# A four-layer kernel on one core: output buffers, the place of the first unit's scans, and the place of layer 2's image copies

## The chip, the cores and the metric

The kernel runs on one core of one Trainium2 chip. Times are microseconds on the device, from the core's first to its last instruction, and the metric is the median over runs. The engines are TensorE (PE in the profile; PEld is its loading of weights), VectorE (DVE), ScalarE (ACT), GpSimd (POOL) and SyncE (SP), which here only issues DMAs. Each engine works through its own instructions in the order of the program; semaphores make one wait for another.

## The reference

The input is float32, two images of 64 channels and 96 x 96 pixels. Four layers follow one another:

- Layer 0: attention over all 9216 pixels of an image with 1x1 convolutions around it, then a batch norm and the residual.
- Layer 1: two depthwise convolutions (3x1 and 1x3) and the input summed, a 1x1 convolution, batch norm and relu; then a layer norm over channels and one Mamba block over the sequence of all 9216 pixels, and a residual.
- Layer 2: Mamba blocks over short sequences of 96 pixels, first down the columns and then along the rows, each forward and backward, with an RMS norm ahead and a joining linear map and residual after.
- Layer 3: a 3x3 filter per group of channels, whose weights come from the image's mean through a tanh, and the residual.

The Mamba block is the core of it, for 128 inner channels and 16 states each:

```
x, z = split(in_proj(norm(u)))
x    = silu(causal_conv4(x) + conv_b)
dt, B, C = split(x_proj(x));  dt = softplus(dt_proj(dt) + dt_b)
h[t] = exp(dt[t] * A) * h[t-1] + dt[t] * B[t] * x[t]      # 128 x 16 states
y    = (sum over states of h * C  +  D * x) * silu(z)
out  = out_proj(y)
```

## The kernel before, in words

The whole image stays on the chip in two tiles, `xa` and `xb`, of 128 partitions (2 images x 64 channels) and 9216 elements. Layer 0 (`layer0_direct`) uses both; afterwards `xb` is the image that layers 1 and 2 read and write in place, and the start of `xa` is carved up (`Carver`) for small tables.

Layers 1 and 2 are one stream of *units* (`layers1_2` builds the list, `Mamba.run` emits it). A unit is one Mamba block over 768 pixels. Layer 1 has 24 units: 12 pieces of each image, one after the other, and the state is carried from piece to piece (`u.carry`). Layer 2 has 96: 24 pairs for the columns, then 24 pairs for the rows; a pair is the forward and the backward block on the same eight sequences. The pair shares its norm, which belongs to the first unit (`u.norm.unit is u`), and one output matmul, `tail`, which belongs to the second. In both layers the first unit of a pair is an even one, counted from 0, and the second an odd one.

A unit has 16 *steps* of scans. The 128 x 16 states are dealt out as 16 turns of 128 rows; a step takes two turns of half a unit, 384 pixels. For one step:

- `read` (L846) fetches `spread`: two DMAs of 384 KB from `rows` in device memory, where `step_write` (L825) put `dt` and `dt * x`. It is issued five steps ahead.
- `decay` (L853) makes `h = exp(dt * A)`, two ACT instructions, three steps ahead.
- `inputs` (L863) makes `dt * x * B` on DVE into a PSUM tile `place`; two steps' `inputs` are issued together at the even step.
- `scan` (L878 in layer 2, L874 in layer 1) is DVE's scan; then GpSimd multiplies by `C` (L879).
- `gather` (L888; L885 begins each half) adds the turns into the PSUM tile `y` on PE, two or three steps later.

`B` is one PSUM tile for half a unit. `shared` (L857) makes it on PE: at step 6 for the second half of the unit, and at step 14 for the first half of the next. It waits until the last `inputs` of the old half has read the tile, and the next `inputs` waits for it.

Everything else of a unit is a *piece*, and the table `PIECES` is an order written out by hand: (offset, name) puts the piece `offset` steps after the unit's step 0. Offsets of -51 to -6 make ready for the scans, 10 to 27 come after. So at each step the program has pieces of up to five units, and offset modulo 16 is the step at which a piece stands. Within a step come the fetch, the decay, the inputs, scan, `B`, gathers, then the pieces that read PSUM (`reads`), then the others. The pieces that matter here:

- `norm_square` at -49 (step 15): in layer 2 two ACT copies of the image (L714, one for each half of the partitions) and ACT's square of the copy (L715); in layer 1 the square and one copy of a matmul's result. `norm_mean` at -47 (step 1) is PE's mean of it (L693), and needs the PSUM tile `mm` that most pieces share.
- `silu` at -22 (step 10), with a table load on each side; `step_mm` at -21 (step 11); `step_read` at -19, `step_exp` at -18, ACT's pieces of the softplus; GpSimd's `step_kept`, `step_sum`, `step_dt` and `step_u` from -17 to -9 (L806 to L816), and `step_write` at -6.
- `c_read` at -15 (step 1): ACT takes `C` out of `mm` (L832).
- `y_half` at 10 and `y_read` at 18: ACT copies a half of `y` into the output tile `yg` (L892, L895); `yg` has two buffers. `y_gate` at 19 multiplies by the gate on GpSimd (L898).
- `tail_0` and `tail_1` at 25 and 26 (steps 9 and 10): PE's output matmuls, which read `yg` of both units of the pair, one half each; `tail_read` at 27 (step 11) writes the image (L921, L924).

The first unit's preparing pieces are emitted ahead of the table (`if offset < 0` in `run`), with layer 1's first relu chunks (`first`, L199 and L200). The table then starts at step -51 of the first unit, so pieces of units 1, 2 and 3 stand ahead of the first unit's scans.

`other` hands out, two calls to each unit at steps 3 and 5, the rest of layer 1's relu chunks and the preparation of layer 2's weights (`mamba_weights`, `joined`).

Of the kernel before, what the change touches and what calls it, by code (L numbers as in the profile page):

```python
# [19 lines left out]
FP = mybir.dt.float32  # L20
# [5 lines left out]
P = 128  # L26
# [45 lines left out]
def setup(ctx, tc, x, cols, mats, dtw):  # L72

    nc = tc.nc
    const = ctx.enter_context(tc.tile_pool(name="const", bufs=1))
    big = ctx.enter_context(tc.tile_pool(name="big", bufs=1))
    k = SimpleNamespace(tc=tc, nc=nc, const=const)

    k.mats = const.tile([P, NMAT], FP, name="mats")
    k.cols = const.tile([P, NCOL], FP, name="cols")  # L80
    k.dtw = const.tile([DT_RANK, NMAMBA * P], FP, name="dtw")
    first = MAT_AT["g_b"][1]
    nc.scalar.dma_start(out=k.mats[:, :first], in_=mats[:, :first])
    nc.scalar.dma_start(out=k.cols, in_=cols)
    nc.scalar.dma_start(out=k.mats[:, first:], in_=mats[:, first:])
    nc.scalar.dma_start(out=k.dtw, in_=dtw)
    k.xa = big.tile([P, L], FP, name="xa")
    k.xb = big.tile([P, L], FP, name="xb")


    half, step = L // 2, L // 6
    own, other = rows_of(0), rows_of(1)
    for i in range(0, half, step):
        nc.sync.dma_start(out=k.xa[own, i : i + step], in_=x[own, i : i + step])
        nc.sync.dma_start(out=k.xb[other, half + i : half + i + step], in_=x[own, half + i : half + i + step])
    nc.sync.dma_start(out=k.xa[other, :half], in_=x[other, :half])
    nc.sync.dma_start(out=k.xb[own, half:], in_=x[other, half:])
    nc.sync.dma_start(out=k.xa[:, half:], in_=x[:, half:])

    k.ident = const.tile([P, P], FP, name="ident")  # L100
    make_identity(nc, k.ident)

    k.mean_c = const.tile([P, P], FP, name="mean_c")
    nc.vector.memset(k.mean_c, 0.0)
    for b in range(B):
        nc.vector.memset(k.mean_c[rows_of(b), rows_of(b)], 1.0 / C)

    k.mean = const.tile([P, 1], FP, name="mean")
    nc.vector.memset(k.mean, 1.0 / C)
    k.mean = k.mean.to_broadcast([P, P])  # L110
    k.eps = const.tile([P, 1], FP, name="eps")
    nc.vector.memset(k.eps, EPS)
    k.minus = const.tile([P, 1], FP, name="minus")
    nc.vector.memset(k.minus, -1.0)

    k.col = lambda name, rows=slice(0, P): k.cols[rows, COL_AT[name][0] : COL_AT[name][1]]
    k.mat = lambda name, rows=slice(0, P): k.mats[rows, MAT_AT[name][0] : MAT_AT[name][1]]
    return k
# [409 lines left out]
def mamba_tables(k, pool):  # L528

    nc = k.nc
    G = P // 8
    t = SimpleNamespace()

    t.member = pool.tile([P, 8], FP, name="member")
    nc.vector.reduce_sum(t.member, k.ident.rearrange("p (g i) -> p i g", i=8), axis=AX.X)
    t.group = pool.tile([P, 2, G], FP, name="group")
    for j in range(2):
        nc.vector.reduce_sum(t.group[:, j], k.ident.rearrange("p (g i) -> p g i", i=8), axis=AX.X)  # L540

    t.turned = pool.tile([P, G, G], FP, name="turned")
    two = t.group.rearrange("p j g -> p (j g)")
    for n in range(G):
        nc.vector.tensor_copy(t.turned[:, n], two[:, G - n : 2 * G - n])

    pair = pool.tile([P, 2, P], FP, name="pair")
    nc.vector.tensor_copy(pair, k.ident.unsqueeze(1).to_broadcast([P, 2, P]))
    pair = pair.rearrange("p j c -> p (j c)")
    t.gather = [pair[:, P - 8 * n : 2 * P - 8 * n] for n in range(G)]  # L550

    t.centre = pool.tile([P, 2, C], FP, name="centre")
    for j in range(2):
        nc.vector.tensor_add(t.centre[:, j], k.ident[:, :C], k.ident[:, C:])
        nc.vector.tensor_scalar_add(t.centre[:, j], t.centre[:, j], -1.0 / C)
    t.centre = t.centre.rearrange("p j c -> p (j c)")
    return t


def scratch(t, pool):  # L560

    t.placed = pool.tile([P, D_STATE, 8], FP, name="placed")
    t.rates = pool.tile([P, P // 8, P // 8], FP, name="turned_rates")


def mamba_weights(k, w, pool, product, tables, i):

    nc = k.nc  # L570
    G = P // 8


    a = pool.tile([P, D_STATE], FP, name=f"A{i}")
    nc.scalar.activation(a, k.col(f"A_log{i}"), AF.Exp)
    nc.vector.tensor_scalar_mul(a, a, -1.0)
    nc.vector.tensor_mul(
        tables.placed,
        tables.member.unsqueeze(1).to_broadcast([P, D_STATE, 8]),
        a.unsqueeze(2).to_broadcast([P, D_STATE, 8]),  # L580
    )
    p = product(tables.placed.rearrange("p s i -> p (s i)"), tables.group[:, 0], P, G)
    yield
    nc.vector.tensor_mul(tables.rates, tables.turned, p.unsqueeze(1).to_broadcast([P, G, G]))  # L584
    w.rates = pool.tile([P, G], FP, name=f"rates{i}")
    nc.vector.reduce_sum(w.rates, tables.rates, axis=AX.X)
    in_w = k.mat(f"in_w{i}")
    if i:
        nc.vector.tensor_scalar_mul(in_w, in_w, k.col(f"norm_w{i}"))
    yield  # L590
    conv_w = k.col(f"convd_w{i}")
    w.taps = pool.tile([P, D_CONV, P], FP, name=f"taps{i}")
    for j in range(D_CONV):
        p = product(conv_w[:, j : j + 1].to_broadcast([P, P]), k.ident, P, P)
        yield
        nc.vector.tensor_mul(w.taps[:, j], in_w[:, :P], p)
        yield
    x_w = k.mat(f"x_w{i}")
    low = pool.tile([DT_RANK, P], FP, name=f"low{i}")
    p = product(x_w[:, :DT_RANK], k.ident, DT_RANK, P)  # L600
    yield
    nc.vector.tensor_copy(low, p)
    yield
    p = product(low, k.dtw[:, bass.ts(i, P)], P, P)
    yield
    w.step = pool.tile([P, P], FP, name=f"step{i}")
    nc.vector.tensor_copy(w.step, p)
    w.direct = pool.tile([P, P], FP, name=f"direct{i}")
    nc.vector.tensor_scalar_mul(w.direct, k.ident, k.col(f"Dp{i}"))
    bc = pool.tile([P, 2, D_STATE, 8], FP, name=f"bc{i}")  # L610
    for j in range(2):
        at = DT_RANK + j * D_STATE
        nc.vector.tensor_copy(bc[:, j], x_w[:, at : at + D_STATE].unsqueeze(2).to_broadcast([P, D_STATE, 8]))
    w.gate_w = in_w[:, P:]
    w.bc = [bc[:, j].rearrange("p s i -> p (s i)") for j in range(2)]
    w.conv_b, w.dt_b = k.col(f"convd_b{i}"), k.col(f"dt_b{i}")
    w.out_w = k.mat(f"out_w{i}")
    yield


class Mamba:
# [79 lines left out]
            u.p = self.mm([(self.t.centre[rows_of(u.b)], self.halves(u.image))])  # L701

    def norm_square(self, u):
        if u.norm.unit is not u:
            return
        u.norm.x = self.work("xn", D_CONV - 1 + CH)
        u.sq = self.work("sq", bufs=1)
        x = u.norm.x[:, D_CONV - 1 :]
        if u.carry:
            self.nc.scalar.activation(u.sq, u.p, AF.Square)  # L710
            self.nc.scalar.copy(x, u.p)
        else:
            for j in range(2):
                self.nc.scalar.copy(x[rows_of(j)].rearrange("p (n t) -> p n t", n=u.image.shape[1]), u.image)  # L714
            self.nc.scalar.activation(u.sq, x, AF.Square)  # L715

    def norm_mean(self, u):
        if u.norm.unit is u:
# [169 lines left out]
            self.nc.tensor.matmul(self.y, lhsT=self.t.gather[n], rhs=rhs, start=False, stop=stop)  # L888

    def y_half(self, u):  # L890
        u.y = self.work("yg")
        self.nc.scalar.copy(u.y[:, :HALF], self.y)  # L892

    def y_read(self, u):
# [21 lines left out]
    def tail_read(self, u):  # L916
# [10 lines left out]


    PIECES = (
        (-51, "norm_centre"),  # L930
        (-49, "norm_square"),
        (-47, "norm_mean"),
# [34 lines left out]
    def run(self, units, first, n_first, other):  # L967


        for u in units:  # L970
            u.dtu, u.h = {}, {}
        steps = [(u, s) for u in units for s in range(self.STEPS)]
        at = lambda n: steps[n] if 0 <= n < len(steps) else None
        reads = ("y_half", "norm_square", "norm_root", "conv_read", "gate_read", "step_read", "c_read", "tail_read")

        table = [[] for _ in range(self.STEPS)]
# [16 lines left out]
        for n in range(begin, len(steps) + end + 1):  # L993
# [5 lines left out]
            if at(n):  # L999
# [6 lines left out]
                self.scan(u, s)  # L1006
                if s == 6:
                    self.shared(u, 1)
                if s == 14 and at(n + 2):
                    self.shared(at(n + 2)[0], 0)  # L1010
            if n == -1:
                self.shared(units[0], 0)
            for late in self.lates(s):
                if at(n - late):
                    self.gather(*at(n - late))
            for late in (False, True):
                for is_late, offset, name in table[s]:
                    i = (n - offset) // self.STEPS
                    if is_late == late and (0 if n >= 0 else 1) <= i < len(units):
                        getattr(self, name)(units[i])  # L1020
                if s in self.OTHER and n >= 0 and not late:
                    next(other, None)
# [2 lines left out]
def prepare(k, scratch_tile, ps, tag):  # L1025
# [5 lines left out]
        return p  # L1031

    k.tables = mamba_tables(k, k.const)
    scratch(k.tables, Carver(scratch_tile))
    k.weights = [SimpleNamespace() for _ in range(NMAMBA)]
    for _ in mamba_weights(k, k.weights[0], k.const, product, k.tables, 0):
        pass
# [2 lines left out]
def layers1_2(k, pre):  # L1040
# [12 lines left out]
    with ExitStack() as stack:  # L1053
# [12 lines left out]


        carver = Carver(k.xa)
        scratch(k.tables, carver)

        def joined(which, lin_w, to):

# [239 lines left out]
```

## Time and profile before

| | us |
|---|---|
| median of three runs | 7903.27 |
| lowest and highest | 7898.69, 7904.27 |
| the profiled execution, first to last instruction | 7904.9 |
| layer 0 ends, preparing pieces of the first unit start | about 2663.8 |
| first `inputs` on DVE (layer 1) | 2734.5 |
| first `inputs` of layer 2, columns | 3774.4 |
| first `inputs` of layer 2, rows | 5847.1 |
| last scan of layer 2 | 7823.4 |

Shares of the span that the engines were busy: PE 89%, DVE 85%, ACT 66%, POOL 60%, over all four layers together. The stages have different limits, so the prediction reads windows. A line of the windows has the stretch, its length, then for PE, PEld, DVE, ACT and POOL the busy time and in brackets the number of instructions, then TensorE's granted clock, the DMA engines' busy share and GB/s. A line of the waits is: who waited (engine, tile, line), for whom, the total, how often, and the longest. A line of the timeline is: start, length, engine, line, operation, tiles and shapes, how many were merged, and in square brackets the idle time of the engine before it and what ended it.

### The profile page before, as it was taken

The page shows a single profiled execution, that of the slowest core. Times are in us where ns is not written, and L with a number is a line of the kernel's source. Part 1 is how long each engine was busy: PE and PEld are TensorE (multiplying, and loading weights), DVE is VectorE, ACT ScalarE, POOL GpSimd, SP SyncE. Part 2 cuts the span into 40 slices and gives each one's busy share as a digit, 9 for nine tenths or more (in the row PEclk, how much of TensorE's full clock was granted, in tenths as well). Part 3 has the DMA queues.
Part 4 walks back from the last instruction along what each step waited for, and adds up shares of the span by engine and source line. Part 5 has one row for each costly group of instructions (what it writes and reads, how often), then busy time and mean ns, then how long its engine had stood idle before and what let it go on. Part 6 is the DMA issues. An engine that isn't in the chain of part 4 may idle for free. (4 is left out here: it accounts for less than half of the span.)

```text
span 7904.9 us, 82275 instructions
## 1 busy us (share of the span) xinstructions
PE 7033.6 (89%) x24578; PEld 3098.9 (39%) x24578; DVE 6744.4 (85%) x5524; ACT 5205.2 (66%) x6953; POOL 4723.5 (60%) x3146
## 2 busy tenths in 40 slices
PE   9999999999999798888888888888888888888887
PEld 3333333333333244444444444444444444444443
DVE  6666666666666499999999999999999999999999
ACT  4444444444444587777777777777777777777774
POOL 0000000000000299999888889889889999999995
PEclk9999999999999899999999999999999999999999
DMA  1000000000000299999889899999999999999995
GB/s 43 1 1 1 1 1 1 3 5 5 5 3 5 105 330 322 328 325 329 321 325 333 315 331 334 332 329 337 330 325 351 345 348 347 336 350 342 344 342 209
DMA packets 593806, 1726.06 MB, mean 218 GB/s; under 512 B 65988, under 2 KB 67140, under 8 KB 592840
## 3 DMA queue, kind: packets, MB, share of 16 engines
q1 hardware_dynamic: 591904, 1717.68, 60.4%
q8 instruction: 196, 3.21, 0.2%
q10 hardware_dynamic: 1448, 3.05, 0.1%
q14 instruction: 258, 2.11, 0.1%
HBM read 1522.68 MB, written 197.79 MB: 218 GB/s over the span
## 5 line engine op out<-in xcount | busy, mean ns | idle before, releaser
L879 POOL TENSOR_TENSOR h<-h,C 128x768 f32<-128x768 f32 x1920 | 3454.0, 1818 | 339.2 <-DVE h L878 304.6
L888 PE MATMUL y<-h,pair 128*128 128x384 f32 x7680 | 2803.3, 508 | 135.1 <-POOL h L879 134.5
L878 DVE TENSOR_TENSOR_SCAN h<-h,place 128x768 f32<-128x768 f32 x1536 | 2606.9, 1738 | 10.8 <-ACT h L853 10.7
L888 PEld LDWEIGHTS y<-h,pair 128*128 128x128 f32 x7680 | 1499.1, 199 | 1335.4 <-POOL h L879 297.7
L311 ACT ACTIVATE e<-f_exp 128x1536 f32<-128x1536 f32 x864 | 1206.4, 1448 | 1224.4 <-PE f_exp L301 1224.4
L853 ACT ACTIVATE h<-spread,xa 128x384 f32<-128x384 f32 x3072 | 1722.5, 607 | 395.0 <-DMA spread<-rows 363.4
L367 DVE TENSOR_TENSOR acc_e<-acc_e,e 128x1536 f32<-128x1536 f32 x792 | 1390.2, 1755 | 683.5 <-ACT e L311 644.6
L863 DVE TENSOR_TENSOR place<-spread,B 128x768 f32<-128x768 f32 x1920 | 1735.0, 951 | 199.6 <-PE B L857 126.7
L340 POOL TENSOR_TENSOR xa<-xa,t_att 64x512 f32<-64x512 f32 x36 | 45.3, 1259 | 2612.0 <-ACT t_att L338 2612.0
L318 PE MATMUL y_att<-e,xb 128*64 128x512 f32 x5184 | 1243.6, 601 | 0.0
L301 PE MATMUL f_exp<-theta,phi 64*128 64x512 f32 x5184 | 1234.5, 607 | 1.0 <-DVE xb L284 0.5
L301 PEld LDWEIGHTS f_exp<-theta,phi 64*128 64x128 f32 x5184 | 466.9, 186 | 754.1 <-issue 460.2
L874 DVE TENSOR_TENSOR_SCAN h<-h,state,place 128x384 f32<-128x384 f32 x768 | 716.4, 1003 | 0.0
L318 PEld LDWEIGHTS y_att<-e,xb 128*64 128x64 f32 x5184 | 341.5, 136 | 830.5 <-issue 829.2
L853 ACT ACTIVATE h<-spread,rates 128x384 f32<-128x384 f32 x768 | 433.8, 608 | 90.6 <-DMA spread<-rows 72.8
L885 PE MATMUL y<-raw,xa 128*128 128x384 f32 x384 | 219.0, 659 | 217.2 <-ACT yg L895 189.8
L671 PE MATMUL mm<-raw,xa 128*128 128x384 f32 x768 | 290.6, 502 | 86.0 <-ACT xb L924 85.9
L766 ACT ACTIVATE raw<-conv,cols 128x768 f32<-128x768 f32 x120 | 108.2, 901 | 280.3 <-PE conv L761 218.9
L806 POOL TENSOR_TENSOR kept<-dtu,kept 128x768 f32<-128x768 f32 x120 | 218.2, 1818 | 100.1 <-ACT kept L799 99.8
L761 PE MATMUL conv<-xn,xa 64*128 64x384 f32 (+3 forms) x1536 | 270.2, 490 | 6.9 <-DVE xa L584 3.0
L892 ACT COPY yg<-y 128x384 f32<-128x384 f32 x120 | 57.4, 478 | 290.9 <-PE mm L671 199.4
L857 PE MATMUL B<-raw,xa 128*128 128x384 f32 x384 | 170.7, 526 | 83.9 <-DVE place L863 83.9
(206 smaller groups left out, 5412.2 us busy)
## 6 DMA issues: line engine op xcount, KB each, us to landing
spread<-rows SPq DMA_DIRECT2D x3840, 384.0 KB, 5.6
rows<-dtu SPq DMA_DIRECT2D x240, 768.0 KB, 6.4
image<-pre SPq DMA_DIRECT2D x11, 384.0 KB, 2.3
xb<-image SPq DMA_DIRECT2D x11, 384.0 KB, 6.7
xa<-in_x SPq DMA_DIRECT2D x1, 2304.0 KB, 22.3
out<-xa ACTq DMA_DIRECT2D x7, 240.0 KB, 2.0
out<-xa SPq DMA_DIRECT2D x1, 1200.0 KB
xa<-in_x SPq DMA_DIRECT2D x3, 384.0 KB, 10.9
```

The lines of the kernel that those rows point to most:

```text
L301: nc.tensor.matmul(fs[j // 3][:, bass.ts(j % 3, NB)], lhsT=phi[at, bass.ts(m // 2, P)], rhs=theta[at, bass.ts(i, NB)], start=True, stop=True,)
L311: nc.scalar.activation(e, f, AF.Exp)
L318: nc.tensor.matmul(y[rows_of(m % 2)], lhsT=g[:, m, :], rhs=es[j // 3][:, bass.ts(j % 3, NB)], start=m < 2, stop=m >= KEYS - 2,)
L367: nc.vector.tensor_add(acc, acc, e)
L671: self.nc.tensor.matmul(o, lhsT=lhsT, rhs=x, start=n == 0, stop=n == len(terms) - 1)
L761: self.nc.tensor.matmul(p3[:, :, o], lhsT=lhsT, rhs=x3[:, :, i], **flags)
L853: self.nc.scalar.activation(h[:, bass.ts(q, HALF)], dt, AF.Exp, scale=u.w.rates[:, n : n + 1])
L863: self.nc.vector.tensor_mul(bx, x, self.B.unsqueeze(1).to_broadcast([P, 2, HALF]))
L874: nc.vector.tensor_tensor_scan(h[:, at], h[:, at], bx[:, at], state[:, q : q + 1], ALU.mult, ALU.add)
L878: nc.vector.tensor_tensor_scan(h[:, way], h[:, way], bx[:, way], 0.0, ALU.mult, ALU.add)
L879: nc.gpsimd.tensor_mul(h2, h2, u.C[:, bass.ts(half, HALF)].unsqueeze(1).to_broadcast([P, 2, HALF]))
L888: self.nc.tensor.matmul(self.y, lhsT=self.t.gather[n], rhs=rhs, start=False, stop=stop)
```

## The change

Three things are changed.

*A third buffer for the output tile.* `yg` gets three buffers in place of two, so `y_half` writes to a tile that the pair before no longer reads. To make room in the on-chip memory, the table `turned` goes from the permanent pool into the scratch space, and is made again when that space moves into `xa`; and of the small weights `dtw` only the first block is loaded at the start, the other four into `xa` when layer 1 begins.

*The first unit's scans a unit sooner.* An empty place is put after the first unit in the list that the table is laid over. The pieces of all later units move 16 steps back, seen from the first unit's scans, so fewer of them stand ahead of these scans; between the first unit's scans and the second's are 16 steps without scans.

*Image copies at two other steps.* In layer 2 the two image copies leave `norm_square` and become pieces of their own: `image_0` at -56 (step 8), and `image_1` with the square at -52 (step 12). The table starts at -56 now.

```diff
-    k.dtw = const.tile([DT_RANK, NMAMBA * P], FP, name="dtw")
+    first_dtw = const.tile([DT_RANK, P], FP, name="dtw")
+    k.dtw, k.dtw_in = lambda i: first_dtw, dtw
...
-def scratch(t, pool):
+def scratch(k, t, pool):
+    G = P // 8
+    t.turned = pool.tile([P, G, G], FP, name="turned")
+    two = t.group.rearrange("p j g -> p (j g)")
+    for n in range(G):
+        k.nc.vector.tensor_copy(t.turned[:, n], two[:, G - n : 2 * G - n])
...
     def norm_square(self, u):
...
         if u.carry:
+            u.norm.x = self.work("xn", D_CONV - 1 + CH)
+            u.sq = self.work("sq", bufs=1)
             self.nc.scalar.activation(u.sq, u.p, AF.Square)
-            self.nc.scalar.copy(x, u.p)
-        else:
-            for j in range(2):
-                self.nc.scalar.copy(x[rows_of(j)].rearrange("p (n t) -> p n t", n=u.image.shape[1]), u.image)
-            self.nc.scalar.activation(u.sq, x, AF.Square)
+            self.nc.scalar.copy(u.norm.x[:, D_CONV - 1 :], u.p)
+
+    def image_copy(self, u, j):
+        if u.norm.unit is u and not u.carry:
+            x = u.norm.x[rows_of(j), D_CONV - 1 :].rearrange("p (n t) -> p n t", n=u.image.shape[1])
+            self.nc.scalar.copy(x, u.image)
+
+    def image_0(self, u):
+        if u.norm.unit is u and not u.carry:
+            u.norm.x = self.work("xn", D_CONV - 1 + CH)
+        self.image_copy(u, 0)
+
+    def image_1(self, u):
+        self.image_copy(u, 1)
+        if u.norm.unit is u and not u.carry:
+            u.sq = self.work("sq", bufs=1)
+            self.nc.scalar.activation(u.sq, u.norm.x[:, D_CONV - 1 :], AF.Square)
...
-        u.y = self.work("yg")
+        u.y = self.work("yg", bufs=3)
...
     PIECES = (
+        (-56, "image_0"),
+        (-52, "image_1"),
         (-51, "norm_centre"),
...
+        units = [units[0], None, *units[1:]]
         steps = [(u, s) for u in units for s in range(self.STEPS)]
-        at = lambda n: steps[n] if 0 <= n < len(steps) else None
+        at = lambda n: steps[n] if 0 <= n < len(steps) and steps[n][0] else None
...
-                if s == 14 and at(n + 2):
-                    self.shared(at(n + 2)[0], 0)
-            if n == -1:
-                self.shared(units[0], 0)
+            if s == 14 and at(n + 2):
+                self.shared(at(n + 2)[0], 0)
...
-                    if is_late == late and (0 if n >= 0 else 1) <= i < len(units):
+                    if is_late == late and (0 if n >= 0 else 1) <= i < len(units) and units[i]:
...
         carver = Carver(k.xa)
-        scratch(k.tables, carver)
+        scratch(k, k.tables, carver)
+        dtw = carver.tile([DT_RANK, (NMAMBA - 1) * P], FP)
+        nc.sync.dma_start(out=dtw, in_=k.dtw_in[:, P:])
+        k.dtw = lambda i: dtw[:, bass.ts(i - 1, P)]
```

More of the change, by code (lines that the diff above doesn't have):

```diff
@@ L85, in setup @@
     nc.scalar.dma_start(out=k.mats[:, first:], in_=mats[:, first:])
-    nc.scalar.dma_start(out=k.dtw, in_=dtw)
+    nc.scalar.dma_start(out=first_dtw, in_=dtw[:, :P])
     k.xa = big.tile([P, L], FP, name="xa")
@@ L540, in mamba_tables @@
         nc.vector.reduce_sum(t.group[:, j], k.ident.rearrange("p (g i) -> p g i", i=8), axis=AX.X)
[L542 to L545, printed above, removed]
     pair = pool.tile([P, 2, P], FP, name="pair")
@@ L603, in mamba_weights @@
     yield
-    p = product(low, k.dtw[:, bass.ts(i, P)], P, P)
+    p = product(low, k.dtw(i), P, P)
     yield
@@ L703, in norm_square @@
     def norm_square(self, u):
[L704 to L708, printed above, removed]
         if u.carry:
+            u.norm.x = self.work("xn", D_CONV - 1 + CH)
+            u.sq = self.work("sq", bufs=1)
             self.nc.scalar.activation(u.sq, u.p, AF.Square)
-            self.nc.scalar.copy(x, u.p)
-        else:
-            for j in range(2):
-                self.nc.scalar.copy(x[rows_of(j)].rearrange("p (n t) -> p n t", n=u.image.shape[1]), u.image)
-            self.nc.scalar.activation(u.sq, x, AF.Square)
+            self.nc.scalar.copy(u.norm.x[:, D_CONV - 1 :], u.p)
[12 more added lines that the diff above has]
+            self.nc.scalar.activation(u.sq, u.norm.x[:, D_CONV - 1 :], AF.Square)
     def norm_mean(self, u):
@@ L1033, in prepare @@
     k.tables = mamba_tables(k, k.const)
-    scratch(k.tables, Carver(scratch_tile))
+    scratch(k, k.tables, Carver(scratch_tile))
     k.weights = [SimpleNamespace() for _ in range(NMAMBA)]
```

## The prediction

> **What bounds the kernel now.** I read the windows first, cut where DVE's work changes: the wait ahead of layer 1, layer 1's 24 units of scans, the first and the second half of layer 2 (48 units each).
>
> ```profile
> 2663.80:2734.50 70.70, 45.49 (x102) 18.60 (x100) 0.03 (x1) 41.82 (x49) 13.13 (x10) 0.64 0.37 136
> 2734.50:3774.40 1039.90, 918.76 (x2813) 440.71 (x2814) 1039.14 (x1184) 821.15 (x1248) 993.79 (x930) 0.98 0.91 326
> 3774.40:5847.10 2072.70, 1736.38 (x5220) 876.48 (x5220) 1960.63 (x1575) 1565.09 (x2353) 1838.51 (x1082) 0.94 0.92 328
> 5847.10:7823.30 1976.20, 1680.59 (x5123) 855.62 (x5122) 1930.38 (x1537) 1503.15 (x2342) 1825.07 (x1074) 0.96 0.94 342
> ```
>
> The third busy time is DVE's. In layer 1 it idles 0.8 us of 1039.9: nothing is to be had there but a sooner start. In layer 2 it idles 112.1 and 45.8 us. A layer-2 unit without a stall takes 8 x 5.017 = 40.14 us (two `inputs` and two scans, every 5.017 us in DVE's timeline), so DVE is the bound and only its idle time can be won: 157.9 us, and 70.7 us at the start.
>
> DVE's waits say what ended these gaps, first half, then second half:
>
> ```profile
> DVE place L863 <- PE B L857: 81.0, 49, 3.6
> DVE h L878 <- ACT h L853: 10.1, 17, 0.9
> ```
> ```profile
> DVE place L863 <- PE B L857: 45.1, 32, 3.1
> DVE h L878 <- ACT h L853: 0.7, 1, 0.7
> ```
>
> Together 136.9 us; the rest of the first half's 112.1 is products of the weight preparation (18.6) and one fetch (1.8). I numbered DVE's instructions (16 `inputs` to a unit) and sorted the gaps by step. Nearly all touch the odd unit, the second of its pair: 33 gaps of 48.5 us at its step 0, 39 of 71.7 us at its step 8, and 18 waits for ACT at step 3, 10.7 us. Even units have 11 gaps at step 8, 6.1 us.
>
> So the matmul `B` is late twice a pair. ACT's timeline in an even unit (steps 8 to 12) shows where the first comes from:
>
> ```profile
> 4588.24 1.12 ACT L853 ACTIVATE h<-spread,xa 128x384 f32<-128x384 f32 x2
> 4593.95 0.48 ACT L892 COPY yg<-y 128x384 f32<-128x384 f32 x1 [4.58 <-PE mm L671]
> 4594.44 1.28 ACT L775 ACT_TABLE_LOAD   x1
> ...
> 4599.56 1.55 ACT L924 ACTIVATE xb<-mm,cols 64x768 f32<-64x768 f32 x1
> ```
>
> `y_half` (L892) stands 4.58 us for the tail's matmuls of the pair before, which still read the output buffer that it overwrites (two buffers). Silu, the decays and `tail_read` (L924) queue behind it. PE's `step_mm` waits for L924 (85.9 us in 46 waits over layer 2), and `B` for the next unit is behind that in PE's order. The second is in PE's timeline, across steps 1 to 6 of the odd unit:
>
> ```profile
> 4616.57 1.65 PE L693 MATMUL mm<-sq,mean 64*128 64x384 f32 x4 [4.17 <-ACT C L832]
> 4618.15 1.65 PE L885 MATMUL y<-raw,xa 128*128 128x384 f32 x2
> 4619.59 6.20 PE L888 MATMUL y<-h,pair 128*128 128x384 f32 x16
> 4625.72 2.81 PE L761 MATMUL conv<-xn,xa 64*128 64x384 f32 x16
> 4628.46 0.91 PE L857 MATMUL B<-raw,xa 128*128 128x384 f32 x2
> ```
>
> `norm_mean` waits 4.17 us for ACT's `c_read`, since ACT has been busy without a gap from 4593.95 on, with both image copies (L714, 3.10 us) and the square at step 15. Gathers and `conv` pile up, `B` starts at 4628.46, and DVE, free at 4626.7, waits 2.72 us.
>
> **What the Trainium skill says.** "PSUM — Partial Sum Buffer", section Engine vs sequencer instructions: ScalarE's queue is strict FIFO and matmuls start in program order. The trace agrees: nothing of ACT runs in the 4.58 us. "Perfetto Trace Analysis", section Optimization Strategy: a bubble that repeats on the engine which should be saturated can mean too few buffers. Here it repeats on ACT, 47 times in 48 pairs (199.4 us). "SBUF — State Buffer", section Door 1: The DMA port swizzle: 16-byte lines, each crossing to a new line costs. Agrees: an image copy is 1546 ns in the first half (elements 96 apart), 830 ns in the second (contiguous).
>
> **Part by part.**
>
> *Third output buffer.* The buffer that `y_half` takes was last read a pair sooner; the 4.58 us wait falls to that for the gather before it (about 1 us at most, as in odd units). No work is added.
>
> *Image copies at steps 8 and 12.* ACT's work per pair is unchanged: 2 x 1.55 + 0.84 = 3.9 us, moved ahead of `y_half` and of `step_read`. By itself that does not bring `c_read` forward, as the copies stay in front of it; it is the removed wait that does, and the first copy now fills idle time. Working the example through with its own durations: the copy runs at 4586.5, of whose 1.55 us gate_read's old wait absorbs 1.07, so `y_half` ends near 4591.0 in place of 4594.4; silu's 4.1 us and two decays bring `tail_read` to 4596.2-4597.8 in place of 4601.1; then PE's own backlog counts, and `step_mm` starts at 4599.4 in place of 4601.17. `B` for the odd unit is 1.8 us sooner. The mean gap at step 0 is 48.5 / 33 = 1.5 us, but some are near 3. I take 75%: 36 us.
>
> After the second copy and the square, `step_read` ends near 4604.2 in place of 4604.6, so PE's next matmul does not suffer, and `c_read` is done near 4612.8 in place of 4616.5: 3.5 us or so sooner. PE's wait there averages 160.6 / 46 = 3.5 us. `B` moves forward by up to that, against a mean gap of 71.7 / 39 = 1.8 us. I take 90%: 65 us. The 10.7 us of step 3 go too, since the two copies no longer stand between `B` and the decays. The 6.1 us of even units I leave. Sum: 36 + 65 + 11 = 112 us, at most 137, at least the step-3 waits and half of the 71.7: 47.
>
> *First unit sooner, then an empty place.* Its first fetches are issued at 2707.99 and 2709.83 and land by 2713.4, but its decays queue on ACT behind unit 1's silu and step pieces; DVE starts at 2734.53. After, only unit 1's norm (ACT to 2709.8) is ahead, so DVE starts at about 2713.4, held 1.1 us between the first two steps by the fetches (2715.45), and ends its unit near 2757.6 (42.9 us of scans). Then unit 1 must be ready, and its pieces no longer run ahead. GpSimd's products for step 15 end near 2759.9; behind these in its queue are kept, log, yg, dt, u: 5 x 1.82 us, to 2769.0; row write, read and landing took 2713.36 - 2703.16 = 10.2 us in the first unit. Unit 1 starts at 2779.2, with its second step held to 2781.3, against 2777.86 before. ACT's silu of unit 2 (4 us) and PE's conv fit in that gap. So 21 us are gained and then spent again: net +2.5 us, from -3 (a sooner landing) to +8 (another wait in the chain).
>
> *Buffers and tables.* Sixteen copies of `turned` a second time lie in DVE's 70.7 us of idleness, and the smaller `dtw` loads beside setup; the second one is 8 KB among fetches and wanted units later. Nothing. Weight products shift from odd to even units, where PE is less late; the 18.6 us may shrink, I count nothing.
>
> Sum: 7903.3 - 112 + 2.5 = 7794.
>
> **The rivals.**
>
> *DMA becomes the bound.* A unit fetches and writes (32 x 384 + 2 x 768) KB = 14.16 MB; at 40.2 us that is 352 GB/s, and the page's slices of both layers hold 315 to 351. ACT already waits 361.9 us for fetches in layer 2. Were 345 GB/s the most, a unit takes 41.0 us: 96 x 41.0 + 38 us of weight work = 3974 in place of 4049, so 7903 - 75 + 2.5 = 7831. For it: "DMA: Bandwidth & Descriptors", section Bandwidth, gives 358 GB/s as the HBM limit of a core. Against it: the unit from 7083.83 ran at 361 GB/s, and units of 40.1 us at 349 and 359 without a stall.
>
> *One chain only.* PE's tail matmuls (6 us in the even unit), not ACT, hold `B` at step 0: gain 65 + 11, so 7830.
>
> *The start pays in full.* If unit 1's chain were shorter by 18 us: 7794 - 22 = 7772. Against it: the five GpSimd products and the row trip are serial.
>
> *Slower.* Unit 1 waits a whole empty unit (2757.6 + 42.8 = 2800.4, +22.5), and ACT's burst at steps 8 to 12 just moves the gaps: 7926. Against it: ACT is 75% busy in layer 2, so the wait removed is real room.
>
> **How the numbers follow.** Forecast 0.52; DMA 0.15; one chain 0.12; full start 0.12; slower 0.09. The range, 7765 to 7842, holds the first four but for their tails (0.08) and leaves the slower case out. Faster 0.89, same 0.02, slower 0.09.
>
> **What would show it.** ACT's wait at `y_half` for the tail's matmuls gone; `norm_mean`'s wait for `c_read` under 1 us; DVE's waits for `B` in layer 2 below 30 us; odd units at 40 to 41 us; the first scans 20 us sooner, then a gap of 20 to 25 us on DVE before the second unit, and layer 1 ending within 8 us of where it did. Wrong would be: waits of the decays for fetches growing until DVE shows them, GpSimd (38 us a unit) standing for ACT and holding the gathers, or a long chain in the empty place.

## The result, and the profile after

The changed kernel takes 7781.11 us (median of 4 runs, 7776.01 to 7792.32) against 7903.77 us (4 runs, 7898.69 to 7916.05): a ratio of 0.9845, 95% interval 0.9827 to 0.9862, so 122.7 us less.

The windows of the kernel after come first: two stretches of its start (to the first scans, and to the second unit), the other 23 units of layer 1, and the two halves of layer 2. The columns are as before: length, then busy time of PE, PEld, DVE, ACT and POOL, the granted clock, DMA's share and GB/s.

```profile
2669.00:2716.90 47.90, 29.53 (x69) 12.22 (x67) 0.02 (x1) 25.41 (x29) 10.42 (x7) 0.71 0.32 120
2716.90:2789.60 72.70, 54.06 (x156) 24.65 (x156) 43.09 (x49) 53.71 (x75) 44.66 (x42) 0.85 0.63 236
2789.60:3798.60 1009.00, 873.55 (x2691) 417.21 (x2692) 998.93 (x1138) 785.40 (x1195) 951.83 (x891) 0.99 0.91 323
3798.60:5762.30 1963.70, 1720.33 (x5219) 859.66 (x5218) 1953.74 (x1572) 1575.73 (x2352) 1836.25 (x1082) 0.96 0.95 346
5762.30:7701.00 1938.70, 1685.78 (x5123) 849.71 (x5122) 1927.40 (x1537) 1518.77 (x2342) 1823.67 (x1074) 0.96 0.95 349
```

Measured to the end of the last scan (7701.6; the last window stops 0.6 us short of it), the halves of layer 2 are 109.0 and 37.0 us shorter, together 146.1. DVE idles 10.0 and 11.3 us in them, where it idled 112.1 and 45.8: 136.6 us of the gain is idle time won. The rest, 9.4 us, is DVE's busy time. The weight preparation runs about a unit sooner, so three of its instructions, 3.4 us, now lie in layer 1 (1572 instructions in place of 1575 in the first half); where the other 6 us come from stays open. Layer 2 starts 24.3 us later (3798.65 in place of 3774.40), and what follows the last scan is the same to 0.1 us. The sum, -146.1 + 24.3 - 0.1 = -121.9, is the difference of the two profiled spans (7904.9 and 7783.0).

DVE's list of waits, first half of layer 2, then second half:

```profile
DVE place L878 <- PE B L872: 6.8, 11, 1.1
DVE xa L579 <- ACT xa L578: 1.7, 1, 1.7
DVE xa L599 <- PE mm L660: 1.2, 1, 1.2
```
```profile
DVE place L878 <- PE B L872: 10.5, 11, 1.6
DVE place L878 <- DMA spread<-rows: 0.7, 1, 0.7
```

The waits for `B` were 81.0 and 45.1 us in 81 pieces; 17.3 us in 22 are left, and those of the decays for ACT (10.8 us) are gone. Numbered by step as before: step 0 of the odd unit 0.2 us (48.5 before), step 8 of the odd unit 6.7 us (71.7), step 8 of the even unit 10.5 us (6.1).

ACT's timeline in the same even unit that the prediction read (now about 12 us sooner), from its step 8 on:

```profile
4574.94 1.55 ACT L719 COPY xn<-xb 64x768 f32<-64x768 f32 x1
...
4580.10 0.48 ACT L907 COPY yg<-y 128x384 f32<-128x384 f32 x1 [0.89 <-PE y L903]
...
4585.78 1.61 ACT L939 ACTIVATE xb<-mm,cols 64x768 f32<-64x768 f32 x1
4587.19 1.08 ACT L868 ACTIVATE h<-spread,xa 128x384 f32<-128x384 f32 x2
4588.30 1.55 ACT L719 COPY xn<-xb 64x768 f32<-64x768 f32 x1
4589.89 0.85 ACT L730 ACTIVATE sq<-xn 128x768 f32<-128x768 f32 x1
```

`y_half` (L907) waits 0.89 us in place of 4.58, and for the gather before it. The first copy stands ahead of it, the second between `tail_read` (L939) and the `step_read` of the next unit. PE's timeline in the odd unit of the pair:

```profile
4601.41 0.91 PE L696 MATMUL mm<-sq,mean 64*128 64x384 f32 x4 [1.28 <-ACT C L847]
4602.80 0.91 PE L900 MATMUL y<-raw,xa 128*128 128x384 f32 x2 [0.47 <-ACT yg L910]
4603.55 4.03 PE L903 MATMUL y<-h,pair 128*128 128x384 f32 x12
...
4609.23 2.81 PE L776 MATMUL conv<-xn,xa 64*128 64x384 f32 x16
4611.97 0.91 PE L872 MATMUL B<-raw,xa 128*128 128x384 f32 x2
```

`norm_mean` waits 1.28 us in place of 4.17, and `B` of step 8 starts 17.98 us after the unit's first scan work (4593.99); it was 22.47 (4628.46 - 4605.99). DVE needs it after four step pairs, 4 x 5.017 = 20.07 us.

Not all went that way. Two stretches got longer. The first is the empty place in the table; here lines of all engines around its end are put together in order of time:

```profile
2780.80 2.39 PE L674 MATMUL mm<-raw,step 128*128 128x384 f32 x4 [1.62 <-ACT xb L936]
2781.57 1.11 ACT L868 ACTIVATE h<-spread,rates 128x384 f32<-128x384 f32 x2
2784.97 2.92 PE L674 MATMUL mm<-xb,centre 64*128 64x384 f32 x4 [1.78 <-ACT dtu L808]
2787.82 1.65 PE L872 MATMUL B<-raw,bc 128*128 128x384 f32 x2
2789.50 1.83 DVE L878 TENSOR_TENSOR place<-spread,B 128x768 f32<-128x768 f32 x2 [27.77 <-DMA spread<-rows]
```

The last line puts DVE's 27.77 us down to a fetch. But ACT's decays read the fetched rows from 2781.57 on, 7.9 us before DVE starts. What came last is `B`, at 2787.82, behind `step_mm` and `norm_centre` of the third unit in PE's order. The second stretch is the passage from layer 1 to layer 2, in the 21st unit of layer 1:

```profile
3649.27 0.19 POOL L751 COPY xn<-xn 128x3 f32<-128x3 f32 x1
3649.42 1.55 POOL L752 TENSOR_TENSOR xn<-xn,sq 128x768 f32<-128x768 f32 x1
3649.49 1.51 ACT L719 COPY xn<-xb 64x768 f32<-64x768 f32 x1 [12.44 <-POOL xn L751]
```

The first image copy of layer 2's first pair takes an `xn` buffer that a norm of layer 1 still holds; GpSimd's L751 is its last reader. ACT stands 12.44 us with everything behind it, and DVE waits 9.1 us in that unit (1.70 + 1.85 us for decays, 5.56 us for `B`).

### The profile page after: what moved, and what is told of

It is laid out like the page before. It is cut to its first block, busy times and chain, and to the rows that moved or that the text cites. A ratio compares the mean times of both kernels' runs of the same rounds, so it can differ in the third digit from the quotient of the medians.

```text
span 7783.0 us, 82242 instructions
## 1 busy us (share of the span) xinstructions
PE 7018.7 (90%) x24578; PEld 3071.8 (39%) x24578; DVE 6738.6 (87%) x5540; ACT 5232.9 (67%) x6953; POOL 4720.4 (61%) x3146
## 4 chain that ended last, share of the span: by engine, by line
PE 11%; DMA 10%; issue 9%; ACT 8%; POOL 7%; DVE 5%; SPq 1%; DVEq 0%; ACTq 0%; POOLq 0%
DMA spread<-rows 7%; PE y L903 6%; POOL h L894 5%; ACT h L868 4%; DMA rows<-dtu 3%; DVE place L878 2%; DVE h L893 2%; PE mm L674 1%; PE conv L776 1%; POOL dtu L827 1%; PE y L900 1%; DVE xa L1231 1%; POOL dtu L831 1%; ACT L791 1%; ACT L790 0%
## 5 line engine op out<-in xcount | busy, mean ns | idle before, releaser
L868 ACT ACTIVATE h<-spread,xa 128x384 f32<-128x384 f32 x3072 | 1754.6, 608 | 501.1 <-DMA spread<-rows 466.7
L903 PEld LDWEIGHTS y<-h,pair 128*128 128x128 f32 x7680 | 1478.0, 197 | 1400.5 <-POOL h L894 422.9
L913 POOL TENSOR_TENSOR yg<-yg,raw 128x768 f32<-128x768 f32 x120 | 218.0, 1817 | 2.2 <-ACT yg L910 2.2
## 6 DMA issues: line engine op xcount, KB each, us to landing
xa<-in_x SPq DMA_DIRECT2D x3, 384.0 KB, 11.3
```

Source lines behind the costliest of these rows:

```text
L868: self.nc.scalar.activation(h[:, bass.ts(q, HALF)], dt, AF.Exp, scale=u.w.rates[:, n : n + 1])
```

## Experiments

No kernel here leaves out or changes any part of the computation. Units are numbered from 0; "unit 1" is the second. Where a gap is given by step, it is the sum of DVE's idle times before the instructions of that step, from the profiled run.

### e1: the third output buffer alone

The change without the image copies and the empty place (the moved tables stay):

```
-        (-56, "image_0"),
-        (-52, "image_1"),
...
-        units = [units[0], None, *units[1:]]
```

with `norm_square` as before, and `u.y = self.work("yg", bufs=3)` kept.

> The third output buffer alone (with the moves of tables that make room for it); image copies at step 15 and the order of the first unit as before. Theory 1, the buffer carries the gain of layer 2: the wait of y_half for the tail's matmuls goes, so everything behind it on ScalarE is some 4 us sooner in every pair; VectorE's waits in layer 2 fall from 157.9 us to 35 or less, and the time to 7775 to 7800. Theory 2, the copies carry it: waits above 100 us, 7860 or more. Layer 0: if the 4.2 us by which its first exponential came late in the changed kernel belong to the second place of the table called turned, they show here; if they are chance or the gap's, not.

Measured: 7852.16 us (7845.42 to 7869.17), ratio 0.9928 (0.9915 to 0.9942). The time is between the two; DVE idles 115.3 us in layer 2, as theory 2 has it. Its waits in the first half of layer 2:

```profile
PE mm L696 <- ACT C L835: 112.1, 24, 7.1
DVE place L866 <- PE B L860: 49.2, 32, 3.5
ACT yg L895 <- PE y L891: 44.0, 46, 1.5
```

The wait of `y_half` for the tail is gone, and all gaps at step 0 are gone with it (48.5 us to 0). But those at step 8 of odd units are as before (44.8 + 31.0 us in the two halves against 44.7 + 27.0), and `norm_mean` waits for `c_read` longer than before (112.1 us against 100.0). ACT in the pair looked at above shows why:

```profile
4596.29 1.60 ACT L927 ACTIVATE xb<-mm,cols 64x768 f32<-64x768 f32 x1
...
4601.05 0.90 ACT L795 ACTIVATE dtu<-mm,cols 128x768 f32<-128x768 f32 x1 [0.65 <-PE mm L674]
...
4608.07 3.08 ACT L717 COPY xn<-xb 64x768 f32<-64x768 f32 x2
4611.18 0.84 ACT L718 ACTIVATE sq<-xn 128x768 f32<-128x768 f32 x1
...
4614.69 0.77 ACT L835 COPY C<-mm 128x768 f32<-128x768 f32 x1
```

`tail_read` is 3.3 us sooner than before (4599.56), but `step_read` can't start ahead of PE's `step_mm`. ACT's free time has moved from ahead of `y_half` to between `tail_read` and `step_read`, where it is 1.4 us a pair in the first half, in place of 0.1; the trace puts most of it down to decays waiting for fetches (23.2 us in 23 pairs), and 6.3 us to `step_read` waiting for PE. The two copies and the square still stand between `step_read` and `c_read`.

### e2: the image copies alone

The two pieces and their functions in the kernel before, with two output buffers:

```
+        (-56, "image_0"),
+        (-52, "image_1"),
```

> The image copies at steps 8 and 12 alone, two output buffers, first unit as before. Theory 1: the wait of y_half stays, but the first copy now lies inside it (1.5 us in the first half of layer 2, 0.8 us in the second), so c_read is only that much sooner: VectorE's waits in layer 2 fall by 30 to 50 us, and about 9 us are lost where layer 1 passes to layer 2, since the first copy waits for a buffer there: 7865 to 7885. Theory 2: 7800 or less.

Measured: 7853.18 us (7847.03 to 7858.95), ratio 0.9929 (0.9916 to 0.9943), again between, 12 us below theory 1's range. In the first half of layer 2:

```profile
ACT yg L904 <- PE mm L671: 104.0, 23, 5.1
DVE place L875 <- PE B L869: 58.0, 42, 3.4
PE mm L693 <- ACT C L844: 61.0, 24, 3.1
```

The mirror image: `y_half` waits as before (104.0 us against 103.6) and step 0 keeps its gaps (48.0 us); step 8 of odd units falls from 71.7 to 31.1 us, and step 3 to nothing. About 10 us of it go at the passage between the layers (unit 20 takes 53.5 us in place of 43.4).

### e3: the empty place alone

The kernel before with `None` after its first unit, and the first `B` made in the table:

```
+        units = [units[0], None, *units[1:]]
```

> The empty place alone. Theory 1: first scans 20 us sooner, second unit's scans 7 us later than in the kernel before, since its first B stands on TensorE behind pieces of the third unit; then nothing changes: 7908 to 7914. Theory 2, the head start is kept: 7885.

Measured: 7908.13 us (13 runs, 7897.51 to 7932.24), ratio 1.0006 (0.9996 to 1.0015). The median is where theory 1 put it, but the interval holds no change as well; the trace is what tells. DVE's timeline from the first scans to the second unit:

```profile
2718.39 0.96 DVE L863 TENSOR_TENSOR place<-spread,B 128x768 f32<-128x768 f32 x1 [49.27 <-DMA spread<-rows]
2720.16 0.96 DVE L863 TENSOR_TENSOR place<-spread,B 128x768 f32<-128x768 f32 x1 [0.80 <-DMA spread<-rows]
2789.59 1.83 DVE L863 TENSOR_TENSOR place<-spread,B 128x768 f32<-128x768 f32 x2 [27.41 <-PE B L857]
```

The same gap as in the changed kernel, and here the trace names `B`. For a comparison of starts I count from a mark, ACT's first square of a norm after the relu chunks of L200: 2702.72 before, 2707.80 here, 2707.03 in the changed kernel (L202 there). It moves with layer 0's start alone, 2662.7 to 2663.0 us after layer 0's first exponential in these three. From it, unit 2 starts after 124.7 us in place of 117.9: by these two profiles the empty place costs 6.8 us.

### e4: the change without the empty place

```
-        units = [units[0], None, *units[1:]]
```

and the first `B` made ahead of the table again.

> The changed kernel without the empty place. Theory 1: 7 us faster than the changed kernel, 7774, second unit's scans at 2782 (2778 and layer 0's 4.2). Theory 2, the empty place is worth its head start: 7795 to 7800.

Measured: 7767.38 us (7764.18 to 7778.66), ratio 0.9824 (0.9811 to 0.9838): the side of theory 1, by 13.7 us in place of 7. DVE's waits for `B`, first half of layer 2, then second half:

```profile
DVE place L878 <- PE B L872: 3.9, 6, 0.9
```
```profile
DVE place L878 <- PE B L872: 4.6, 5, 1.9
```

Unit 2 starts at 2819.9 in place of 2832.3. Against the mark that is 114.6 us in place of 125.3. Single profiles scatter here: the seven kernels without the empty place have 114.6 to 120.3 us, 117.3 on average, and the three that have it and keep `B` where it was (e3, e6 and the changed kernel) 124.7 to 126.4, so the empty place costs about 8 us.

With e1 and e2 this settles the main sum. DVE's idle time in layer 2 is 157.9 us before, 115.3 with the buffer alone, 92.6 with the copies alone and 11.2 with both. The two win 42.6 and 65.3 us by themselves and 146.7 together, 38.8 more than their sum; some 30 of these lie at step 8 of the odd units (gaps of 71.7, 75.8, 31.1 and 5.4 us).

### e5: `B` of the second unit earlier

```
-            if s == 14 and at(n + 2):
+            if s == 14 and at(n + 2) and n + 2 != 2 * self.STEPS:
                 self.shared(at(n + 2)[0], 0)
+            if n == self.STEPS + 1:
+                self.shared(units[2], 0)
```

> The changed kernel with the second unit's first B made at step 1 of the empty place in place of its step 14, so that it stands ahead of the third unit's pieces on TensorE. Theory 1, B ended VectorE's 27.8 us gap: the fetched rows had landed at 2781.8, B was made at 2787.8 behind the third unit's step_mm and norm_centre; so the gap shrinks to some 20 us, and the time to 7773. Theory 2, the fetch ended it, as the wait's line says: gap and time unchanged, 7781.

Measured: 7770.80 us (7765.14 to 7774.74), ratio 0.9829 (0.9815 to 0.9842). DVE's timeline:

```profile
2781.17 0.96 DVE L878 TENSOR_TENSOR place<-spread,B 128x768 f32<-128x768 f32 x1 [20.13 <-DMA spread<-rows]
2783.68 0.96 DVE L878 TENSOR_TENSOR place<-spread,B 128x768 f32<-128x768 f32 x1 [1.55 <-DMA spread<-rows]
...
2807.70 1.83 DVE L878 TENSOR_TENSOR place<-spread,B 128x768 f32<-128x768 f32 x2 [3.38 <-PE B L872]
```

So it was `B`: the gap falls from 27.77 to 20.13 us, and now the fetch does end it. Most is given back inside the unit, which waits 1.55 us for its second fetch and 3.38 us for the second `B`. Unit 2 starts 123.8 us after the mark, against 125.3 in the changed kernel: 1.5 us are kept. The other 9 us of the medians' difference are not explained by this edit. The profiled runs put much of them into the second half of layer 2, where the two kernels have the same code and DVE idles 3.3 us here and 11.3 us there.

### e6 and e7: the passage between the layers

The first layer-2 pair makes its first copy at step 12, with the second; all later pairs as in the change. e6 has the empty place, e7 has not.

```
+            u.entry = not u.carry and units[j - 1].carry
...
-        if u.norm.unit is u and not u.carry:
+        if u.norm.unit is u and not u.carry and not u.entry:
```

> The changed kernel, but the very first pair of layer 2 takes its first image copy at step 12 with the second, once. Theory 1: at the passage from layer 1 to layer 2 ScalarE's 12.4 us wait (the copy waits for the buffer of a layer-1 norm that GpSimd reads two steps later) goes, and with it three VectorE waits of 9.1 us in unit 20: 7772. Theory 2, the passage costs as much at another place: 7781.

> The changed kernel without the empty place and with the first pair's copy at step 12. If the two losses are independent: 7767 less 9, 7758. If the passage's loss depends on the empty place: 7767.

Measured: e6 7764.79 us (7759.74 to 7770.56), ratio 0.9820 (0.9807 to 0.9833); e7 7760.61 us (7754.69 to 7765.33), ratio 0.9814 (0.9801 to 0.9828). In e6, lines of two engines in order of time:

```profile
3647.32 0.19 POOL L754 COPY xn<-xn 128x3 f32<-128x3 f32 x1
3647.46 1.55 POOL L755 TENSOR_TENSOR xn<-xn,sq 128x768 f32<-128x768 f32 x1
3648.76 3.06 ACT L719 COPY xn<-xb 64x768 f32<-64x768 f32 x2
```

ACT no longer waits there, and unit 20 takes 43.0 us in place of 52.5. The passage cost the change 9.5 us of that unit, of which 9.1 are DVE's waits named above. The medians differ by 16.3 us, and as with e5 the rest is not explained by this edit. e7 has the lowest median of all kernels here, but its interval overlaps those of e4, e6 and e9: 20.5 us below the changed kernel, with intervals that barely touch, and not shown to be better than those three.

### e8: both copies at step 12

On e4, so that nothing new stands ahead of `y_half`, and 1.5 us more stand ahead of `step_read`:

```
-        (-56, "image_0"),
+        (-52, "image_0"),
```

> The changed kernel without the empty place, both image copies and the square at step 12. Theory 1, ScalarE's free time that the third buffer makes is some 3 us a pair, in two pieces, of which the one at step 8 is worth a copy: with 3.9 us at one step ahead of step_read, step_read is 1 to 1.5 us later, and gaps of about 0.8 us at step 8 of odd units return in the first half of layer 2, 10 to 20 us; less the 9 us of the passage, which step 12 avoids for all: 7768 to 7780. Theory 2, any place ahead of step_read does: 7758.

Measured: 7775.41 us (7767.59 to 7780.48), ratio 0.9832 (0.9819 to 0.9845), as theory 1 has it, and 14.8 us above e7, which loses nothing at the passage either. First half of layer 2:

```profile
DVE place L878 <- PE B L872: 22.0, 21, 2.0
PE mm L696 <- ACT C L847: 68.5, 24, 3.3
```

Against e4 `step_read` moves back from 2.82 to 1.53 us ahead of the odd unit's start, `c_read` from 6.26 to 7.41 us after it, `B` from 18.80 to 20.16 us: just past the 20.07 at which DVE wants it. Gaps at step 8 of odd units come back, 19.7 us in 17 of 24.

### e9: the changed kernel with both mends

The edits of e5 and e6 together.

> The changed kernel with both mends: B of the second unit early in the empty place, and the first copy of layer 2's first pair at step 12. Theory 1: the empty place in itself is a cost that the early B does not remove. In the profile with early B alone, the third unit starts 123.8 us after layer 0's last work (125.3 with the change as it is, 114.6 to 117.4 without the empty place), because unit 1 then waits 3.4 us at its step 8. So early B is worth about 2 us on top of the mended passage (7764.8): about 7763, behind the kernel without the empty place and with the mended passage (7760.6). Theory 2: the two mends add up by their medians: 7781.1 - 16.3 - 10.3 = 7754.5, ahead of it.

Measured: 7762.07 us (7755.83 to 7771.15), ratio 0.9822 (0.9809 to 0.9836), as theory 1 has it. The earlier `B` takes 2.7 us off e6's median, within its spread; the 10 us of e5's median do not come again.

### e10: both copies at step 8

On e7:

```
-        (-52, "image_1"),
+        (-56, "image_1"),
```

> Third output buffer, no empty place, mended passage, and both image copies at step 8, ahead of y_half. Theory 1: what counts is that the copies fill the time which the third buffer frees ahead of y_half (4.58 us, of which both take 3.1), and that nothing stands between tail_read and step_read: step_read starts sooner than with the copies at 8 and 12 (-2.7 us against the odd unit's start), norm_mean does not wait longer, no gaps at step 8 of odd units: 7757 to 7763. Rival: y_half and with it silu, decays and tail_read come 1.5 us later, so that step_mm and B for step 0 of the odd unit are late again: gaps at step 0 of 0.5 us or more in half the pairs, 7775 to 7790.

Measured: 7776.19 us (7773.04 to 7780.98), ratio 0.9838 (0.9825 to 0.9851): the rival's number, but not for its reason. Gaps at step 0 of odd units are 3.5 us in 9 pairs, where the rival needed half a microsecond or more in half of them, and `norm_mean`'s wait for `c_read` is the shortest of all (18.4 us in 24). What came back is the passage: my edit moved the first pair's copies to step 8 as well.

```profile
3638.06 1.54 POOL L755 TENSOR_TENSOR xn<-xn,sq 128x768 f32<-128x768 f32 x1
3638.14 3.02 ACT L719 COPY xn<-xb 64x768 f32<-64x768 f32 x2 [13.07 <-POOL xn L754]
```

Unit 20 takes 55.7 us, 12.2 more than in e7 (43.4). Less that, the time would be about 7764, next to theory 1's. So this place for the copies was not tried cleanly, and is not shown to be better or worse than 8 and 12.

## Why the prediction was right, and where it was not

The table gives mean starts in the first half of layer 2, in us from the first scan work of the odd unit: `tail_read`, `step_read`, `c_read`, and PE's `B` of step 8, over the 24 pairs of each profiled run (23 for `tail_read`).

| kernel | tail_read | step_read | c_read | B of step 8 | gaps at step 0, odd | gaps at step 8, odd |
|---|---|---|---|---|---|---|
| before | -6.75 | -3.13 | 9.64 | 22.55 | 48.5 | 71.7 |
| e1, buffer | -8.61 | -3.46 | 9.51 | 22.40 | 0 | 75.8 |
| e2, copies | -6.75 | -0.92 | 8.02 | 20.90 | 48.0 | 31.1 |
| e4, both | -9.00 | -2.82 | 6.26 | 18.80 | 0.5 | 5.4 |
| after | -8.77 | -2.70 | 6.27 | 18.81 | 0.2 | 6.7 |

(Gaps are sums over layer 2, in us.)

**Third output buffer: right.** The forecast had `y_half`'s wait at about 1 us at most; it is 50.4 us in 48 in the first half, 1.05 each. `tail_read` comes 2.0 us sooner on average, and step 0 gave 48.3 us in place of the 36 taken; e1 shows that this is the buffer's work alone. The bubble that repeated on ACT was a buffer too few, as the Trainium skill's page "Perfetto Trace Analysis", section Optimization Strategy, says it can be; the page speaks of the engine that should be saturated, which here is DVE and not ACT. The mend by itself brought 54.7 us (7852.16 against 7906.83 in the same series), not what the wait's 199.4 us suggest.

**Image copies: the size right, the cause wrong.** `c_read` was to come 3.5 us or so sooner; it comes 3.4 us sooner (9.64 to 6.27). The 65 us taken for step 8 are what was measured (71.7 to 6.7), and the 11 of step 3 too. The step that failed is the sentence "By itself that does not bring `c_read` forward, as the copies stay in front of it; it is the removed wait that does". Against the odd unit's start, which is what step 8 is measured by, the removed wait alone (e1) brings `c_read` forward by 0.1 us and the copies alone (e2) by 1.6 us. In e1 `tail_read` is 3.3 us sooner, counted from the even unit's start. But 1.4 us of that the odd unit uses to start sooner itself (41.2 us after the even one in place of 42.6), which is the gain at step 0. Most of the rest turns into idleness of ACT ahead of `step_read`, since ACT takes its work in order and nothing from behind has been put there. And copies put there without free time push `step_read` back by 2.2 us (-3.13 to -0.92). Each edit takes away what limits the other, and that is why 42.6 and 65.3 us make 146.7. Forecast as a sum of two steps, the total came out because both edits were in it, and not because the reason given was right.

**Weight products: missed.** Counted at nothing, "may shrink": their 18.6 us of waits fell to 2.9, so 15.7 us came from here. The reason that the prediction gave, a shift from odd to even units, is not what did it. With the empty place alone (e3), 18.2 us are left, 17.1 of them still in odd units; with the two other edits and no empty place (e4), 2.2 us are left. The copies alone (e2) leave 9.9.

**Even units:** left at 6.1 us; 10.5 now (between 2.9 and 7.2 in e4 to e7 and e9, so not a cost of the change that is shown). The sum over layer 2's idleness is 48.3 + 65.0 + 10.7 + 15.7 - 4.4 and 1.3 of fetches and the like: 136.6, where 112 was taken and 137 named as the most.

**First unit sooner: too cheap.** Forecast +2.5 us, at most +8. The first part held: first scans at 2716.90, which is 9.9 us after the mark, in place of 31.8. The chain of GpSimd's products and the row trip held too: forecast to let unit 1 start at 2779.2, or 2783.5 with layer 0 now 4.3 us later; its rows are read from 2781.57 on. What failed is "ACT's silu of unit 2 (4 us) and PE's conv fit in that gap". These are not all that stands there: `step_mm` waits for ACT's tail and `norm_centre` for ACT's step pieces, and `B` is behind both. Unit 2 starts 7.4 us later against the mark (125.3 and 117.9), and 6.8 in e3. e5 shows that `B` holds the start of unit 1 and that little is won by moving it, since the unit's next needs are as late.

**Missed altogether: the passage.** 9.1 us of waits, shown by e6. The copies were costed as work in a running layer 2; that the first pair takes its buffer seven steps sooner, while a layer-1 norm still holds it, was not looked for.

Layer 2 so starts 24.3 us later: 7.4 us of the empty place, 9.1 of the passage, 4.3 from layer 0 (below), and 3.5 left over. From unit 2 to layer 2, DVE is busy 2.8 us longer, with the three instructions of weight work that moved there (34 in place of 31), and one of that work's instructions waits 0.8 us at 3015.0. The errors have opposite signs: 25 us more won in layer 2's idle time and 9 us less of DVE's busy time in it, 22 us more lost ahead of it. The forecast of 7794 lies 13 us above the result, and that closeness is in part luck.

**Rivals.** DMA as the bound is refuted for this rate: the two halves of layer 2 moved 346 and 349 GB/s, ACT's waits for fetches rose from 361.9 to 464.6 us, and DVE waits 0.7 us for one. One chain only: with the buffer alone (e1) the gaps at step 0 are gone, so PE's tail matmuls did not hold `B` there. The slower case: not seen. The start in full: e5, with `B` out of the way, still has a gap of 20.1 us, so the serial chain is real. One rival that was not named, a higher granted clock of TensorE, does not carry the gain either: in the second half of layer 2 the clock is 0.96 before and after, and DVE's idle time fell from 45.8 to 11.3 us all the same.

**Signs named.** Waits of DVE for `B` below 30 us: 17.3. Odd units at 40 to 41 us: 40.85 and 40.46 on average. First scans 20 us sooner: 17.6 by the clock, 21.9 against the mark. The gap of 20 to 25 us was 27.8, layer 1 ended 24.3 us later and not within 8, and `norm_mean` still waits 1.6 us each (38.5 in 24), not under 1.

## What to carry to other kernels

In a queue that runs in order, a removed wait is worth less than its length unless work can be moved into the time it frees: look for the next thing the queue stands for, and for work behind it that could be done ahead. So try two edits to one queue together as well as apart; here each brought about 54 us and both 139.5. When a piece of work is moved earlier, ask of its first instance who holds the buffer that it takes, and of an empty place in a table what is left in order ahead of the first thing needed after it.

## What was not expected of the hardware

- A line's releaser can be wrong by far: 27.77 us were put down to a fetch whose rows another engine had been reading for 7.9 us. The same gap in e3 was put down to `B`. The times of the other operands tell which it was.
- Layer 0 starts unevenly. Its first exponential is at 39.81 us in the kernel before and 39.32, 42.91, 42.58 and 45.12 us in e2, e1, e4 and e3, though e3 has the same code up to there. All later times move with it (the mark: 2702.40 to 2707.80 us). In these five it is later where a weight fetch (`mats`) lands later, at 12.71 to 14.5 us; but e9 has that landing at 14.54 and the exponential at 41.23, so the cause is open. Differences of 5 us between single profiles are to be read against it.
- Kernels with the same code in layer 2 (after, e4, e5, e6, e7, e9) idle there between 10 and 21 us in one profiled run each, the changed kernel most (21.3 us, the others 10.4 to 13.2). By their medians e4, e5 and e6 lie 3 to 9 us further below the changed kernel than their edits explain, which may be the same thing. Whether this is phase, set by the start, or scatter is open.
